# A graph-attention layer on one core: the row of reciprocal deviations goes through DRAM

## The chip, the core and the metric

The kernel runs on one core of a Trainium2 chip. A core has five engines that run their own instruction streams in order and meet through semaphores: TensorE (PE in the profile: matrix products and transposes, results in PSUM banks), VectorE (DVE), ScalarE (ACT), GpSimd (POOL) and SyncE (SP, which only issues transfers here). Sixteen DMA engines move data between DRAM and the on-chip memory SBUF, which has 128 partitions. The metric is the device time of one execution in microseconds (us); lower is better. The median before is 299.23 us over 3 runs (299.14 to 299.44).

## The reference

A graph layer on 384 nodes with 1024 features, 16 heads of 64. What matters here is its head, the layer norm and the three projections:

```python
h = jnp.maximum(_layernorm(x, axis=-1), 0.0)      # (x - mean) / sqrt(var + 1e-5), then relu
q = h @ wq.T + bq;  k = h @ wk.T + bk;  v = h @ wv.T + bv
q2 = (q @ wiq.T + biq)...;  k2 = (k @ wik.T + bik)...;  v2 = (v @ wiv.T + biv)...   # per head
mask = full((N, N), -inf); mask[src, dst] = softplus(edge_type_weights)[edge_type - 1]; diagonal filled
attn = softmax(q2 @ k2.T / 8 + mask);  out = attn @ v2
return x + (out @ wo.T + bo)
```

There are 6528 edges with types 0 to 4. Everything is float32.

## The kernel before

**Precision.** Each float32 operand is split into a rounded high part and a low part, and a product is three matmuls: high by high, high by low, low by high (`mm3`, L367). `split_hi` (L67) makes the high part of a weight chunk on ACT, `split_lo` (L79) the low part on DVE, or on POOL where one is named.

**Layer norm without its division.** The norm is taken apart. `ln_bn` and `ln_mean` (L246, L249) make mean and variance on DVE, `ln_sub` subtracts the mean, and PE transposes the centred rows, so that nodes lie along the free axis; relu and split give `hT`. The division by the standard deviation is left out at that point. Since relu commutes with a positive factor, it can be multiplied in later, on the result of each projection. `ln_root` and `ln_rstd` (L255, L259) make the reciprocal deviation, three columns of 128 (one for each block of nodes; node on the partition). `ln_row` (L266) turns these three columns into a row of 384 that is the same in all partitions, `rrow`: PE transposes each column, read as if it stood 128 times side by side, into one PSUM bank, and ACT copies the bank to SBUF. `evac_row` (L387) then multiplies the PSUM result of a chunk by `rrow` on DVE (L389), ACT adds the bias and rounds (L390), and DVE makes the low part (L391), put off to the next chunk's head by the list `post`.

**Chunks.** The work is a list of 56 weight chunks of 512 KB, numbered by `w`: 0 to 7 are the eight output blocks of v, 8 to 15 those of q, then the inner projection of v, k, and so on. A chunk takes 24 matmuls of 128x384. `slot_head(w)` (L402) runs ahead of each chunk: it splits the high part of chunk w+2 (ACT), empties `pend` (the evacuation of the chunk before), splits the low part of chunk w+2 (DVE), empties `post`, and issues the load of chunk w+5 on SP. `raw` has four buffers, so a load can start once the chunk four before it has been split.

**The first two chunks.** Their matmuls are written out as pieces, because the parts of `hT` and of the weights come in one after the other: chunk 0 high by high, then low by high; in the slot of chunk 1 its high by high, the rest of chunk 0, its low by high, and its high by low in two halves, with `ln_row` and the evacuation of chunk 0 (`flush`) between the halves (L422 to L429). PSUM has eight banks; the tag "g", in which chunks accumulate, has three, so chunk 3 takes chunk 0's bank once its evacuation has read it.

**The mask, beside it.** The mask is built from the edge list by POOL, DVE and DMA while the projections run. `softplus_a`, `softplus_b`, `softplus_c` (L155 to L167) make the four edge weights, `mask_values` (L169) the value of every edge on POOL. `detect(s)` (L442) is called behind each chunk of v and q: it clears one of three tables in DRAM (`table_clear`, L143, a transfer of 576 KB) behind the first three chunks, loads rows of keys, compares them for repeated edges (`mask_detect`, L213, on DVE), makes indices (`mask_index`) and, from the fourth on, scatters two columns of edges at a time (L224, POOL). `softplus_c` and `mask_values` are called by `detect(0)`.

**Order.** All engines' orders are as written in the program, and SP issues every transfer named here in one queue. An instruction that waits holds up all behind it on its engine.

Of the kernel before, what the change touches and what calls it, by code (L numbers as in the profile page):

```python
# [8 lines left out]
F32 = mybir.dt.float32  # L9
F32R = mybir.dt.float32r  # L10
I32 = mybir.dt.int32
AF = mybir.ActivationFunctionType
OP = mybir.AluOpType

N, D, NT, KT, NP = 384, 1024, 3, 8, 8
# [7 lines left out]
def gnn_kernel(ctx: ExitStack, tc: tile.TileContext, x, edges, erows, etw, wq, wk, wv, wiq, wik, wiv, wo,  # L23
# [6 lines left out]
    nc = tc.nc  # L30
# [5 lines left out]
    dram = ctx.enter_context(tc.tile_pool(name="dram", bufs=1, space=bass.MemoryType.DRAM))  # L36
# [7 lines left out]
    def bank(tag):  # L44
        return psum.tile([128, 512], F32, tag=tag, name=tag, bufs={"g": 3, "a": 1}.get(tag, 2))
# [14 lines left out]
    def load(w):  # L60
        if w >= NCH:
            return
        n, m = chunks[w]
        raw[w] = wpool.tile([128, D], F32, tag="raw", name="raw", bufs=4)
        nc.sync.dma_start(raw[w], W[n][m])

    def split_hi(w, dst=None, dve=False):  # L67
        if w >= NCH:
            return
        if dst is None:  # L70
            t = wpool.tile([128, 2, D], F32R, tag="whl", name="whl", bufs=4)
            dst = (t[:, 0, :], t[:, 1, :])
        whl[w] = dst
        if dve:
            nc.vector.tensor_copy(dst[0], raw[w])
        else:
            nc.scalar.activation(dst[0], raw[w], AF.Copy)  # L77

    def split_lo(w, eng=None):  # L79
        if w < NCH:  # L80
            hi, lo = whl[w]
            (eng or nc.vector).tensor_tensor(lo, raw[w], hi.bitcast(F32), OP.subtract)  # L82
# [24 lines left out]
    ident = const.tile([128, 128], F32, name="ident")  # L107
# [35 lines left out]
    def table_clear(g):  # L143

        nc.sync.dma_start(tabs[g][:CELLS, :].rearrange("(j p m) o -> p j (m o)", p=128, m=N),
                          zero[:, None, :].to_broadcast([128, NT, N]))
# [18 lines left out]
    def softplus_c():  # L165
        nc.vector.tensor_tensor(w8[:, 4:8], w8[:, 4:8], w8[:, 0:4], OP.add)
        nc.vector.tensor_scalar(w8[:, 4:8], w8[:, 4:8], 8.0, 1.0e-37, op0=OP.mult, op1=OP.max)  # L167

    def mask_values():  # L169
        t, ty = tmpe[:, 0, :], tmpe[:, 2, :]  # L170
        nc.gpsimd.tensor_scalar(val, ty, 0.0, w8[:, 7:8], op0=OP.is_equal, op1=OP.mult)
        for i in range(4):
            nc.gpsimd.tensor_scalar(t, ty, float(i + 1), w8[:, 4 + i:5 + i], op0=OP.is_equal, op1=OP.mult)
            nc.gpsimd.tensor_tensor(val, val, t, OP.add)
# [17 lines left out]
    def key_load(g, s):  # L192

        if s == 0:
            t = work.tile([128, 2, NT, N], F32R, tag="pt", name="rows")
            krv[g] = t.bitcast(F32).rearrange("p a k n -> p (a k n)")
        c0, c1 = parts(g)[s]
        dst = krv[g][:, s * PA * 128:(s * PA + c1 - c0) * 128]
        for c in range(c0, c1):
            rows[c] = krv[g][:, (s * PA + c - c0) * 128:(s * PA + c - c0 + 1) * 128]  # L200
        nc.sync.dma_start(dst, krow[c0:c1, :].rearrange("c j -> (c j)").partition_broadcast(128))
# [37 lines left out]

    hT = gtile("g1")  # L240
    lnt = work.tile([128, N], F32, tag="e", name="lnt", bufs=EB)
    var, negm, root, vq, inv, rstd = (lnt[:, c:c + NT] for c in (4, 8, 12, 16, 20, 24))
    var = lnt[:, 1:2 * NT:2]
    rrow = work.tile([128, 2, N], F32R, tag="qs", name="rrow").bitcast(F32)[:, 0, :]

    def ln_bn(t, h):  # L246
        nc.vector.bn_stats(lnt[:, 30 + 12 * t + 6 * h:36 + 12 * t + 6 * h], xt[t][:, h * 512:(h + 1) * 512])  # L247
# [18 lines left out]
    def ln_row():  # L266

        ps = bank("t")
        for t in range(NT):
            nc.tensor.transpose(ps[:, t * 128:(t + 1) * 128], rstd[:, t:t + 1].to_broadcast([128, 128]), ident)  # L270
        nc.scalar.activation(rrow, ps[:, :N], AF.Copy)

    def ln_sub(t, c0, c1, eng):
        src, dst = xt[t][:, c0:c1], xn[t][:, c0:c1]
# [97 lines left out]
    def colmm(ps, w, src, k):  # L372
        hi, lo = whl[w]
        mm3(ps[:, :N], hi[:, k * 128:(k + 1) * 128], lo[:, k * 128:(k + 1) * 128],
            src[:, 0, k, :], src[:, 1, k, :], k == 0, k == KT - 1)

    def pieces(ps, w, src, a, b, ks, n=(0, N)):

        for k in ks:
            nc.tensor.matmul(ps[:, n[0]:n[1]], whl[w][a][:, k * 128:(k + 1) * 128], src[:, b, k, n[0]:n[1]],  # L380
                             start=(a == b == k == n[0] == 0), stop=(b == 1 and k == KT - 1))
# [5 lines left out]
    def evac_row(ps, hi, lo, bias):  # L387
        f = work.tile([128, N], F32, tag="e", name="f", bufs=EB)
        nc.vector.tensor_tensor(f, ps[:, :N], rrow, OP.mult)  # L389
        nc.scalar.activation(hi, f, AF.Identity, bias=bias)  # L390
        post.append(lambda: nc.vector.scalar_tensor_tensor(lo, f, bias, hi.bitcast(F32), op0=OP.add, op1=OP.subtract))  # L391

    w = 0
    pend, post = [], []

    def flush(last=False):
        while pend:
            pend.pop(0)()
        while last and post:
            post.pop(0)()  # L400

    def slot_head(w):  # L402
        if w > 0:
            split_hi(w + 2)
        if w != 1:
            flush()
        split_lo(w + 2)
        while post:
            post.pop(0)()
        load(w + 5)  # L410

    def proj(src, dst, bidx, extra=None):
        nonlocal w
        for m in range(8):
            slot_head(w)
            ps = bank("g")
            if w == 0:
                ps0 = ps
                pieces(ps0, 0, src, 0, 0, range(KT), (0, 256))
                pieces(ps0, 0, src, 0, 0, range(KT), (256, N))  # L420
                pieces(ps0, 0, src, 1, 0, range(KT))
            elif w == 1:  # L422
                pieces(ps, 1, src, 0, 0, range(KT))
                pieces(ps0, 0, src, 0, 1, range(KT))
                pieces(ps, 1, src, 1, 0, range(KT))
                pieces(ps, 1, src, 0, 1, range(4))
                ln_row()
                flush()
                pieces(ps, 1, src, 0, 1, range(4, KT))  # L429
            else:  # L430
                for k in range(KT):
                    colmm(ps, w, src, k)
            pend.append(lambda ps=ps, m=m: evac_row(ps, dst[:, 0, m, :], dst[:, 1, m, :],
                                                bc[:, bidx * 8 + m:bidx * 8 + m + 1]))
            if extra:
                extra(m)
            w += 1

    def extra_v(m):
        detect(m)  # L440

    def detect(s):  # L442

        if s == 0:
            softplus_c()
            mask_values()
        if s < NTAB:
            table_clear(s)
        if 3 <= s < 6:
            key_load(1, s - 3)  # L450
        if 9 <= s < 12:
            key_load(2, s - 9)
        detects((0, 3, 6)[s] if s < 3 else 2)
        if s >= 3:
            scatters(2)
        if s == 14:
            biv_load()
# [3 lines left out]
    def detects(n):  # L461
        for i in range(nde[0], min(EC, nde[0] + n)):
            mask_detect(sc_order[i])
            if i + 1 == NTAB * JI[1]:
                mask_index(JI.pop(0), JI[0])
            nde[0] = i + 1

    def extra_q(m):
        detect(8 + m)
# [3 lines left out]
    def scatters(n):  # L473
        for _ in range(n):
            if nsc[0] < EC:
                mask_scatter(nsc[0])
                nsc[0] += 1
# [3 lines left out]
    def biv_load():  # L481
        t = work.tile([128, 2, 2, N], F32R, tag="ks", name="bivt")
        bivs["b"] = t.bitcast(F32).rearrange("p a k n -> p (a k n)")[:, 0:D]
        nc.sync.dma_start(bivs["b"], biv.partition_broadcast(128))

    vT = gtile("g2")
    proj(hT, vT, 2, extra_v)
    qT = gtile("g3")
    proj(hT, qT, 0, extra_q)

    xbd = dram.tile([N, D], F32, name="xbd")
# [24 lines left out]
    for k in range(8):  # L516
        slot_head(w)
        hi, lo = whl[w]
        for t in range(NT):
            for h in range(2):  # L520
                mm3(accs[t * 2 + h], vT[:, 0, k, t * 128:(t + 1) * 128], vT[:, 1, k, t * 128:(t + 1) * 128],
                    hi[:, h * 512:(h + 1) * 512], lo[:, h * 512:(h + 1) * 512], k == 0, k == KT - 1)
        detects(2)
        scatters(2)
        if k == 6:
            mask_fill()
            mask_base()
        if k >= 2:
            residual(k - 2)
        w += 1  # L530
# [11 lines left out]
    def extra_k(m):  # L542
# [5 lines left out]
        if m < 2:  # L548
            residual(m + 6)
    kT = gtile("g2")  # L550
    proj(hT, kT, 1, extra_k)
    flush(True)

# [332 lines left out]
```

## Time and profile before

| | us |
|---|---|
| median of 3 runs (lowest, highest) | 299.23 (299.14, 299.44) |
| the profiled execution | 298.95 |
| its span, first to last instruction | 297.2 |
| PE busy | 291.2 (98%) |
| DVE busy | 202.4 (68%) |
| POOL busy | 155.7 (52%) |
| ACT busy | 153.8 (52%) |
| packets of DMA queue q1, share of 16 engines' span | 56.0% |

Times in a timeline are counted from the span's start. A line of a timeline reads: start, duration, engine, line of the program, operation, output<-inputs, shapes, and in brackets how long the engine had been idle and what ended that. SPq lines are the issues of transfers; their duration is the issue alone, not the transfer. A transfer's end is seen where somebody waited for it. Numbers of buffers are left out of names: `g` stands for PSUM banks of the tag "g" and for the large tiles of activations, `raw` for loaded weights, `whl` for their high and low parts, `tab` for the tables. In a line of windows come the stretch, its length, busy time and number of instructions of each engine, the clock granted to PE, the mean busy share of the DMA engines and GB/s. The chain of waits is followed back from the last instruction; what stands on it decides the end.

### The profile page before, as it was taken

To read this page: it belongs to the slowest core of one execution; us is meant where nothing else is said; L and a number is where in the kernel's file an instruction comes from. 1 tells how busy PE (TensorE), PEld (TensorE's weight loads), DVE (VectorE), ACT (ScalarE), POOL (GpSimd) and SP (SyncE) were. 2 spreads that over 40 slices of the span, in tenths; PEclk is the share of its full clock that TensorE was granted. 3 is DMA by queue.
4 is the path that set the end of the run, shared out by engine and by line. 5 is a ranking of instruction groups with operands and counts; after the bars stand their busy time and mean duration, and the time that the engine had idled before them with its cause. 6 is when DMAs were issued, how large, how long until landed. Compare 5 with 4: busy or idle time off the path is not lost.

```text
span 297.2 us, 4982 instructions
## 1 busy us (share of the span) xinstructions
PE 291.2 (98%) x1654; PEld 276.5 (93%) x1654; DVE 202.4 (68%) x495; ACT 153.8 (52%) x288; POOL 155.7 (52%) x160
## 2 busy tenths in 40 slices
PE   6999999999999999999999999999999999999995
PEld 5999999999988889999999999999999998888884
DVE  4958977766856553888865676868686766696423
ACT  3784644433422222554336677778777767865310
POOL 3774567363857785710033656373746467976210
PEclk9999999999999999999999999999999999999999
DMA  7899864645396648393369784738374656900005
GB/s 279 277 324 398 292 207 131 225 143 212 116 303 202 197 153 289 113 342 112 117 167 261 206 216 115 202 93 223 99 221 121 170 144 176 348 10 0 2 3 209
DMA packets 22377, 55.12 MB, mean 185 GB/s; under 512 B 4816, under 2 KB 8400, under 8 KB 22352
## 3 DMA queue, kind: packets, MB, share of 16 engines
q1 hardware_dynamic: 19968, 52.42, 56.0%
q0 software_dynamic: 2064, 1.80, 2.1%
q10 hardware_dynamic: 320, 0.59, 0.9%
q8 instruction: 13, 0.21, 0.3%
q14 instruction: 12, 0.10, 0.1%
HBM read 40.39 MB, written 4.97 MB: 153 GB/s over the span
## 4 chain that ended last, share of the span: by engine, by line
PE 96%; DVE 1%; DMA 1%; ACT 0%; issue 0%
PE g L370 21%; PE g L368 21%; PE g L369 21%; PE a L758 6%; PE s L721 6%; PE t L741 5%; PE g L380 3%; PE s L369 2%; PE s L370 2%; PE s L368 2%; PE t L370 2%; PE t L369 2%; PE t L368 2%; DMA g<-in_x_dram 1%; DVE lnt L247 1%; PE a L369 1%
## 5 line engine op out<-in xcount | busy, mean ns | idle before, releaser
L368 PE MATMUL g<-g,whl 128*128 128x384 f32 x304 | 103.6, 341 | 0.0
L370 PE MATMUL g<-g,whl 128*128 128x384 f32 x304 | 101.8, 335 | 0.0
L369 PE MATMUL g<-g,whl 128*128 128x384 f32 x304 | 101.5, 334 | 0.0
L224 POOL DMA_INDIRECT tab<-val,idx x51 | 56.1, 1100 | 37.5 <-issue 11.0
L77 ACT ACTIVATE whl<-raw 128x1024 fp32r<-128x1024 f32 x51 | 53.6, 1051 | 29.7 <-PE g L370 21.1
L82 DVE TENSOR_TENSOR whl<-raw,whl 128x1024 fp32r<-128x1024 f32 x41 | 52.6, 1282 | 15.6 <-ACT whl L77 12.4
L736 POOL TENSOR_TENSOR e<-e,s 128x384 f32<-128x384 f32 x48 | 39.3, 829 | 43.1 <-DVE s L735 42.4
L369 PEld LDWEIGHTS g<-g,whl 128*128 128x128 f32 x304 | 57.2, 188 | 0.0
L368 PEld LDWEIGHTS g<-g,whl 128*128 128x128 f32 x304 | 57.1, 188 | 0.0
L370 PEld LDWEIGHTS g<-g,whl 128*128 128x128 f32 x304 | 57.0, 188 | 0.0
L82 POOL TENSOR_TENSOR whl<-raw,whl 128x1024 fp32r<-128x1024 f32 x11 | 26.4, 2398 | 30.8 <-ACT whl L77 28.1
L390 ACT ACTIVATE g<-f,bc 128x384 fp32r<-128x384 f32 x24 | 14.8, 618 | 52.7 <-DVE f L389 41.2
L751 DVE TENSOR_TENSOR pt<-t,pt 128x384 fp32r<-128x384 f32 x48 | 26.4, 549 | 15.3 <-ACT pt L750 15.0
L731 ACT ACTIVATE e<-e,s 128x384 f32<-128x384 f32 x48 | 29.2, 608 | 9.3 <-DVE s L727 8.1
L750 ACT ACTIVATE pt<-t 128x384 fp32r<-128x384 f32 x48 | 23.3, 486 | 13.6 <-PE t L741 13.3
L727 DVE CUSTOM_DVE_ANT_0 e<-s,ma 128x384 f32<-128x384 f32 x48 | 26.4, 549 | 3.6 <-PE s L721 3.4
L721 PE MATMUL s<-ks,qs 128*128 128x384 f32 x96 | 24.7, 338 | 0.0
L741 PE MATMUL t<-ident,e 128*128 128x128 f32 x144 | 23.5, 271 | 0.0
L389 DVE TENSOR_TENSOR f<-g,rrow 128x384 f32<-128x384 f32 x24 | 13.3, 556 | 13.9 <-PE g L370 13.7
L741 PEld LDWEIGHTS t<-ident,e 128*128 128x128 f32 x144 | 18.7, 140 | 3.1
L758 PE MATMUL a<-pt,vhl 128*128 128x384 f32 x96 | 20.8, 351 | 0.0
L721 PEld LDWEIGHTS s<-ks,qs 128*128 128x128 f32 x96 | 17.5, 188 | 0.8
(145 smaller groups left out, 416.2 us busy)
## 6 DMA issues: line engine op xcount, KB each, us to landing
ks<-nat SPq DMA_DIRECT2D x30, 192.0 KB
raw<-in_wv_dram SPq DMA_DIRECT2D x8, 512.0 KB
raw<-in_wq_dram SPq DMA_DIRECT2D x8, 512.0 KB
raw<-in_wiv_dram SPq DMA_DIRECT2D x8, 512.0 KB
raw<-in_wk_dram SPq DMA_DIRECT2D x8, 512.0 KB
raw<-in_wiq_dram SPq DMA_DIRECT2D x8, 512.0 KB
raw<-in_wik_dram SPq DMA_DIRECT2D x8, 512.0 KB
raw<-in_wo_dram SPq DMA_DIRECT2D x8, 512.0 KB
```

The source lines that it names most:

```text
L77: nc.scalar.activation(dst[0], raw[w], AF.Copy)
L82: (eng or nc.vector).tensor_tensor(lo, raw[w], hi.bitcast(F32), OP.subtract)
L224: nc.gpsimd.indirect_dma_start(out=tabs[c // RNG], out_offset=bass.IndirectOffsetOnAxis(ap=idx[:, c:c + 1], axis=0), in_=val[:, c:c + 1], ...
L368: nc.tensor.matmul(ps, lhi, rhi, start=first, stop=False)
L369: nc.tensor.matmul(ps, lhi, rlo, start=False, stop=False)
L370: nc.tensor.matmul(ps, llo, rhi, start=False, stop=last)
L721: nc.tensor.matmul(ps[:, :N], qs[:, o, t * 128:(t + 1) * 128], ks[:, o, s, :], start=(s == 0), stop=(s == 1))
L727: nc.vector.tensor_tensor_reduce(e, st_ps.pop(i)[:, :N], ma[:, t, :], -0.125, 3.0e38, OP.add, OP.min, s[:, 0:1])
L731: nc.scalar.activation(es[i], es[i], AF.Exp, bias=s[:, 0:1], scale=-1.0, accum_out=s[:, 1:2])
L736: nc.gpsimd.tensor_tensor(es[i], es[i], s[:, 2:3].to_broadcast([128, N]), OP.mult)
L741: nc.tensor.transpose(ps[:, k * 128:(k + 1) * 128], es[i][:, k * 128:(k + 1) * 128], ident)
L758: nc.tensor.matmul(ps[:, :N], vhl[:, k, p, 2 * o:2 * o + 2, :], pts[h][:, s, k, :], start=(k == 0 and s == 0), stop=(k == 2 and s == 1))
```

## The change

`ln_row` is made in another way, it stands eight matmuls earlier, and some work that was given out ahead of it or behind it is given out right behind it.

- The three reciprocal columns go to columns 128 to 130 of the small tile `lnt`; columns 128 to 255 are cleared on POOL at the start.
- `ln_row` transposes this 128x128 block once on PE. Its first three rows are copied by DVE from PSUM to SBUF (3x128), written to a DRAM tile `rdram` (1.5 KB), and read back from there into all 128 partitions of `rrow` (192 KB). Both transfers are issued by SP, the second after the first has landed. The copy by ACT (L271) is gone.
- It is called when four of the eight low-by-high matmuls of chunk 1 are given out, and no longer between the halves of the high-by-low ones.
- `softplus_c` and `mask_values` are called there, behind it, and no longer by `detect(0)`.
- The low part of chunk 3 (`split_lo(3)`) and the load of chunk 6 (`load(6)`) are given out there too, and no longer in `slot_head(1)`, which ends after the high part of chunk 3. The evacuation of chunk 0 stays where it was.

In program order this gives, on SP: load of chunk 5, clear of table 0, write of `rdram`, read of `rrow`, load of chunk 6, clear of table 1, load of chunk 7, clear of table 2. On DVE: low part of chunk 2, the 3x128 copy, the two softplus instructions, low part of chunk 3, multiplication of chunk 0 by `rrow`, three comparisons.

```diff
-    var, negm, root, vq, inv, rstd = (lnt[:, c:c + NT] for c in (4, 8, 12, 16, 20, 24))
+    var, negm, root, vq, inv, rstd = (lnt[:, c:c + NT] for c in (4, 8, 12, 16, 20, 128))
     var = lnt[:, 1:2 * NT:2]
     rrow = work.tile([128, 2, N], F32R, tag="qs", name="rrow").bitcast(F32)[:, 0, :]
+    rdram = dram.tile([NT, 128], F32, name="rdram")
+    nc.gpsimd.memset(lnt[:, 128:256], 0.0)
...
     def ln_row():
 
         ps = bank("t")
-        for t in range(NT):
-            nc.tensor.transpose(ps[:, t * 128:(t + 1) * 128], rstd[:, t:t + 1].to_broadcast([128, 128]), ident)
-        nc.scalar.activation(rrow, ps[:, :N], AF.Copy)
+        nc.tensor.transpose(ps[:, :128], lnt[:, 128:256], ident)
+        nc.vector.tensor_copy(lnt[:NT, 256:384], ps[:NT, :128])
+        nc.sync.dma_start(rdram, lnt[:NT, 256:384])
+        nc.sync.dma_start(rrow, rdram.rearrange("t n -> (t n)").partition_broadcast(128))
...
     def slot_head(w):
         if w > 0:
             split_hi(w + 2)
-        if w != 1:
-            flush()
+        if w == 1:
+            return
+        flush()
         split_lo(w + 2)
         while post:
             post.pop(0)()
...
             elif w == 1:
                 pieces(ps, 1, src, 0, 0, range(KT))
                 pieces(ps0, 0, src, 0, 1, range(KT))
-                pieces(ps, 1, src, 1, 0, range(KT))
+                pieces(ps, 1, src, 1, 0, range(4))
+                ln_row()
+                softplus_c()
+                mask_values()
+                split_lo(3)
+                load(6)
+                pieces(ps, 1, src, 1, 0, range(4, KT))
                 pieces(ps, 1, src, 0, 1, range(4))
-                ln_row()
                 flush()
                 pieces(ps, 1, src, 0, 1, range(4, KT))
...
     def detect(s):
 
-        if s == 0:
-            softplus_c()
-            mask_values()
         if s < NTAB:
             table_clear(s)
```

## The prediction

> **What bounds the kernel now.** I read the page's busy shares and its chain first. TensorE (PE) is busy 291.2 of 297.2 us and the chain is 96% PE. Then I read the chain in order of time for the edited place:
>
> ```profile
> PE 291.2 (98%) x1654; PEld 276.5 (93%) x1654; DVE 202.4 (68%) x495; ACT 153.8 (52%) x288; POOL 155.7 (52%) x160
> ...
> 10.41 8.16 PE g L380 x52
> 18.57 0.33 PE t L270 x3
> 18.89 0.71 PE g L380 x4
> ```
>
> From 10.4 us on, PE runs without a pause, so any instruction taken off PE is a gain and any wait put in front of PE is a loss of the same size. The three transposes of the edited function cost 0.33 us on the chain, 0.11 each. The next view is the timeline of PE around the first matmul that needs the edited row in time:
>
> ```profile
> 23.44 0.33 PE L370 MATMUL g<-g,whl 128*128 128x384 f32 x1
> 23.61 0.33 PE L368 MATMUL g<-g,whl 128*128 128x384 f32 x1
> ```
>
> 23.61 is the first matmul of chunk 3. There are three "g" banks, chunks 0, 1 and 2 hold them, so chunk 3 needs chunk 0's bank back. That bank is freed by the multiplication with the reciprocal row, L389 on DVE:
>
> ```profile
> 15.63 1.21 DVE L82 TENSOR_TENSOR whl<-raw,whl 128x1024 fp32r<-128x1024 f32 x1
> 17.97 0.16 DVE L166 TENSOR_TENSOR w<-w 128x4 f32<-128x4 f32 x1 [1.14 <-ACT w L161]
> ...
> 20.44 1.22 DVE L82 TENSOR_TENSOR whl<-raw,whl 128x1024 fp32r<-128x1024 f32 x1 [2.10 <-ACT whl L77]
> 21.58 0.55 DVE L389 TENSOR_TENSOR f<-g,rrow 128x384 f32<-128x384 f32 x1
> ```
>
> It ends at 22.13, so the row has 1.48 us to spare before 23.61. Now the row will come through DMA, so I read what SP's queue does there, when it issues and when others get what it issued:
>
> ```profile
> 12.70 2.70 SPq L65 DMA_DIRECT2D raw<-in_wv_dram  x2
> 15.45 0.89 SPq L145 DMA_DIRECT2D tab<-zero  x1
> 16.87 0.34 SPq L65 DMA_DIRECT2D raw<-in_wv_dram  x1
> 17.26 0.54 SPq L145 DMA_DIRECT2D tab<-zero  x1
> ```
>
> ```profile
> 23.34 1.06 ACT L77 ACTIVATE whl<-raw 128x1024 fp32r<-128x1024 f32 x1 [0.56 <-DMA raw<-in_wv_dram]
> 28.76 0.98 POOL L224 DMA_INDIRECT tab<-val,idx  x1 [0.73 <-DMA tab<-zero]
> ```
>
> The first row holds the loads of chunks 4 (12.70) and 5 (15.06). Chunk 4, issued at 12.70, is only there at 23.34: 10.6 us. The second table clear, issued at 17.26, is there at 28.76: 11.5 us. Between them the queue holds chunk 5, table 0, chunk 6 and table 1, 2 x 0.524 + 2 x 0.590 = 2.23 MB, in 5.42 us: 411 GB/s. The windows agree that the DMA engines are full:
>
> ```profile
> 15.00:18.00 3.00, 3.00 (x19) 3.00 (x18) 1.80 (x7) 2.94 (x5) 1.81 (x4) 1.00 1.03 255
> 18.00:21.00 3.00, 3.00 (x20) 2.96 (x19) 0.87 (x3) 2.77 (x4) 2.28 (x5) 1.00 1.00 359
> 21.00:24.00 3.00, 3.00 (x20) 3.00 (x19) 2.14 (x9) 1.28 (x2) 2.40 (x5) 1.00 1.04 400
> 24.00:27.00 3.00, 3.00 (x19) 3.00 (x18) 2.99 (x6) 1.97 (x3) 0.29 (x1) 1.00 1.05 409
> ```
>
> The last two columns are the DMA engines' share (1 is full) and GB/s. So the changed kernel puts two dependent transfers into a queue that is some ten microseconds deep.
>
> **The change part by part.**
>
> *PE.* Two of three transposes go: 0.22 us off the chain. The one left stands eight matmuls earlier: 18.41 - 8 x 0.174 = 17.0, after the reciprocals (15.53), so it waits for nothing. The cleared columns are a 128x128 memset on POOL; one such at 1.33 took 0.20 us, and POOL next has work at 5.73 after 3.15 idle: nothing.
>
> *ACT and DVE.* ACT loses L271 (0.47), with 1.39 idle behind it: nothing. DVE gains a 3x128 copy, between its rows of 128x4 (0.17) and 128x384 (0.55), put at 0.3. It runs from 17.3 in DVE's idle 1.14 before L166, ends about 17.6, and delays nothing. Softplus end and edge values keep their releaser (ACT's logarithm, ending 17.94), so their move costs nothing; nor does that of chunk 3's low part, released by ACT at 20.40 as before. It still stands ahead of the multiplication on DVE, so chunk 3's weights are ready at 21.66.
>
> *The write of the row.* SP issues it about 17.6, behind chunks 4 and 5 and table 0. Upper bound of its landing: the last DMA engine is through with chunk 4 at 23.34, then with 1.11 MB more at 0.405 MB per us, 2.75 us: 26.1. Lower bound: SP had issued 6.67 MB up to and with table 0, and the windows have moved that sum at 22.6, so an average engine is done then. (For chunk 4 the same sum gives 19.7 against 23.34 seen: some engines lag by 3.7.) I take 26.1, because each wait in this stretch ended with the last engine.
>
> The Trainium skill (DMA: Bandwidth & Descriptors, "Why a DMA increments its semaphore by 16 and not by 1") says that such a DMA runs only on as many engines as divide its slowest dimension, three for three rows, and counts only these. No row here has so few rows to show it; by the page the write would land with those three engines, early unless one of them lags, and the sum would be near 302.8 instead.
>
> *The broadcast read.* SP waits for the write before it issues this. Issue to use, nearest rows: the small store of the keys, 8.78 to 10.69, 1.91 us, and a 256 KB store whose follower waits for it, 90.10 to 92.83, 2.73 us. I take the middle, 2.3. So the row is there at 26.1 + 2.3 = 28.4. Ends: 28.8 at 2.73; and 26.6 if the write lands early, since the read has 128 rows and still queues behind table 0 on the lagging engines (26.1, plus its own 0.2 MB, 0.5 us).
>
> *What then waits.* DVE's multiplication starts 28.4, ends 28.95, PE starts chunk 3 about 29.0 in place of 23.61: **5.4 us** (3.6 to 5.8). PE would have been free at 23.4, so the 0.22 saved goes into the pause.
>
> *What is queued behind the two waits.* On SP, chunk 6, table 1, chunk 7 and table 2 wait behind the read: issued from about 26.5 in place of 16.87. Chunk 6 is used 8.43 us after the multiplication (30.01 against 21.58), so now at 36.8, ten microseconds after its issue into an emptied queue (the first load of such a size took 3.3): nothing. Scatters start 5.1 after it (26.71), now 33.5; table 1's clear, 0.2 + 0.52 + 0.59 MB after 26.2, is there by 32: nothing. On DVE three comparisons, an index pair, chunk 1's multiplication and the low parts of chunks 4 and 5 wait. From L389's start to the end of chunk 5's low part DVE took 30.58 - 21.58 = 9.00, of which 0.83 was a wait for POOL's edge values, done by then: 8.17. PE reaches chunk 5 0.6 + 2 x 4.17 = 8.93 after the row. So DVE is in time by 0.76 us, and no second stop follows. ACT, behind its bias step, has chunk 4's high part in time for DVE by about 0.1.
>
> Sum: +5.4 against the profiled run's 298.95, which lies 0.28 under the median of 299.23: **304.6 us** by the median.
>
> **The rivals.**
>
> *The row comes by fewer engines (302.8).* Same stop, but the write lands at 22.6 to 24 and only the read is held by the lagging engines: row at 26.6, chunk 3 at 27.2, +3.6. For it: three rows are few. Against it: nothing in the trace has fewer than all.
>
> *The stop also costs TensorE its pace (306.5).* At the start PE runs 20 transposes in 4.27 us, later three in 0.49: the slow stretch lost about 4.27 - 20 x 0.11 = 2 us. A PE pause of 0.98 us (before 6.68) did not bring the slow pace back; one of 3.7 to 5.6 is not in the trace. Bounds 0 and 2 us, so 304.6 + 1.9.
>
> The Trainium skill (TensorE: Matmul & The Clock Gate, "Part 1: The HAM clock gate") has PE fall to half clock after an idle window of about 3.4 us that runs free. By it a pause of 5.6 us holds a whole window about two times in three, and one of 3.7 hardly ever.
>
> *The other side: the small transfers pass the queue (299.0).* If the write and the read took 1.9 us each, as the keys' store did, the row would be there at 21.4, DVE would start at 21.66 as before, and only the 0.22 us gain is left. It decides at: row by 22.8, so both transfers within 5.2 us of 17.6, where their neighbours take 10.4 and 11.5. Against it: the keys' store had 0.2 MB ahead of it (2.77 issued, 2.6 moved), and the read must use engines that are still busy with chunk 4 at 23.
>
> **How the numbers follow.** In-order stop at full pace 0.40, 304.6 (its own range 304.2 to 305.1, by 1.91 and 2.73 for the read); fewer engines 0.27, 302.8; slow pace after the stop 0.26, 306.5 (from 304.7 to 307); passing the queue 0.05, 299.0; something worse, such as DVE missing chunk 5 too, 0.02. The range 302.3 to 307.0 leaves out the last two and the far end of the slow pace. About 0.2%, 0.6 us, is what can be told from no change: the passing case (-0.2) is mostly within it. Faster 0.01, same 0.04, slower 0.95.
>
> **What would show it.** Right: DVE idle from 21.7 to 26 or later before the first L392 with a DMA of the row as releaser; a PE gap of 3.5 to 5.6 us before chunk 3; SP's broadcast read issued 22.7 to 26.2, chunk 6's load right behind it; no other PE gap until 285. The transposes of PE would take 0.11 instead of 0.33. Matmul spacing after the gap tells the pace: 0.174 is full, about 0.35 slow. Wrong: the read issued before 20.5, or a row that lands within 5 us of 17.6; also a second stop at chunk 5, 6 or 7.

## The result, and the profile after

The changed kernel takes 307.38 us (median of 4 runs, 307.09 to 307.65) against 299.34 before: a ratio of 1.026, 95% interval 1.0244 to 1.0277. It is slower by 8.0 us where 5.4 were forecast, and 0.4 us above the top of the range. The profiled execution is the one of 307.65, span 305.9.

The page's first lines and its row of the clock granted to TensorE, in 40 slices of 7.6 us:

```profile
PE 294.8 (96%) x1652; PEld 280.2 (92%) x1652; DVE 202.2 (66%) x496; ACT 153.6 (50%) x287; POOL 156.0 (51%) x161
...
PEclk9998799999999999999999999999999999999999
```

PE has two instructions fewer and is busy 3.6 us longer: somewhere it works slower. The clock row says where, slices four and five (22.9 to 38.2 us). The chain of waits between 18 and 34 us, start and length of each piece:

```profile
18.45 0.12 PE t L271
18.60 0.04 DVE lnt L272
...
18.91 6.06 DMA rdram<-lnt
24.98 4.72 DMA rrow<-rdram
29.73 0.57 DVE f L392
30.30 0.14 issue
30.43 0.66 PE g L371
31.09 0.32 PE g L372
```

Before, this stretch of the chain was PE alone. Now it leaves PE for the two transfers and comes back through the multiplication. What SP issued, and how long DVE stood:

```profile
18.91 0.33 SPq L273 DMA_DIRECT2D rdram<-lnt  x1
24.98 0.34 SPq L274 DMA_DIRECT2D rrow<-rdram  x1
25.42 0.38 SPq L65 DMA_DIRECT2D raw<-in_wv_dram  x1
```

```profile
29.73 0.56 DVE L392 TENSOR_TENSOR f<-g,rrow 128x384 f32<-128x384 f32 x1 [7.40 <-DMA rrow<-rdram]
```

And PE's timeline around the stop:

```profile
24.50 0.34 PE L373 MATMUL g<-g,whl 128*128 128x384 f32 x1
30.43 0.66 PE L371 MATMUL g<-g,whl 128*128 128x384 f32 x1 [5.59 <-DVE f L392]
30.89 0.52 PE L372 MATMUL g<-g,whl 128*128 128x384 f32 x1
31.21 0.52 PE L373 MATMUL g<-g,whl 128*128 128x384 f32 x1
...
34.41 0.40 PE L371 MATMUL g<-g,whl 128*128 128x384 f32 x1
34.65 0.33 PE L372 MATMUL g<-g,whl 128*128 128x384 f32 x1
34.83 0.33 PE L373 MATMUL g<-g,whl 128*128 128x384 f32 x1
```

Starts lie 0.173 apart before 24.50 and after 34.65, and 0.32 between. From these rows the two executions' spans can be set against each other. Chunk 3 would have begun at 24.50 + 0.17 = 24.67, 1.06 later than the 23.61 of before. The stop is 30.43 - 24.67 = 5.76 (the 5.59 in the bracket is counted from the last matmul's end, 24.84; "idle" below is counted like that). The 13 matmuls from 30.43 to 34.65 took 4.22 in place of 13 x 0.1735 = 2.26, so the slow pace cost 1.96. Together 8.78, where the spans differ by 305.9 - 297.2 = 8.7. Nothing is lost after 35 us, and nothing is won back.

The 1.06 comes from the start of the run and not from the edited place. In this execution the third block of x came 0.7 us later (its statistics start at 7.85 in place of 7.14), and the first transposes kept the slow pace of the start until 10.3 us, so chunk 0's first matmul is at 11.50 in place of 10.16. Whether the change has to do with that is asked below.

### The profile page after: what moved, and what is told of

Read it like the earlier page. It is cut to its first block, busy times and chain, and to the rows that moved or that the text cites. A ratio compares the mean times of both kernels' runs of the same rounds, so it can differ in the third digit from the quotient of the medians.

```text
span 305.9 us, 4984 instructions
## 1 busy us (share of the span) xinstructions
PE 294.8 (96%) x1652; PEld 280.2 (92%) x1652; DVE 202.2 (66%) x496; ACT 153.6 (50%) x287; POOL 156.0 (51%) x161
## 4 chain that ended last, share of the span: by engine, by line
PE 93%; DMA 5%; DVE 1%; ACT 0%; issue 0%
PE g L371 20%; PE g L373 20%; PE g L372 20%; PE a L764 6%; PE s L727 6%; PE t L747 5%; PE g L383 2%; DMA rdram<-lnt 2%; PE s L372 2%; PE s L373 2%; PE s L371 2%; DMA rrow<-rdram 2%; PE t L373 2%; PE t L372 2%; PE t L371 1%; DMA g<-in_x_dram 1%
## 5 line engine op out<-in xcount | busy, mean ns | idle before, releaser
L371 PEld LDWEIGHTS g<-g,whl 128*128 128x128 f32 x304 | 57.8, 190 | 5.9 <-issue 5.9
L372 PEld LDWEIGHTS g<-g,whl 128*128 128x128 f32 x304 | 57.8, 190 | 0.0
L373 PEld LDWEIGHTS g<-g,whl 128*128 128x128 f32 x304 | 57.6, 190 | 0.0
```

Of the source, the lines that this page charges most:

```text
L371: nc.tensor.matmul(ps, lhi, rhi, start=first, stop=False)
L372: nc.tensor.matmul(ps, lhi, rlo, start=False, stop=False)
L373: nc.tensor.matmul(ps, llo, rhi, start=False, stop=last)
```

## Experiments

Two theories of the loss. **The wait**: only the time from the write's issue to the read's landing counts, by a stop of PE before chunk 3, and the slow pace follows from that stop. **Rivals**: the moved work costs something; the loads that SP holds back behind the read cost something; the slow pace has a cause of its own. Within the wait, what makes the write and the read take 6.1 and 4.7 us is asked separately. In the three groups of runs the kernel before took 299.71, 299.80 and 299.55 us, and each ratio is to the kernel before of its own group.

### Is it the way through DRAM, and there the wait alone?

**Moves without the way through DRAM** (e1_moves_only): `ln_row` as before, all else as changed.

```diff
-        nc.tensor.transpose(ps[:, :128], lnt[:, 128:256], ident)
-        nc.vector.tensor_copy(lnt[:NT, 256:384], ps[:NT, :128])
-        nc.sync.dma_start(rdram, lnt[:NT, 256:384])
-        nc.sync.dma_start(rrow, rdram...partition_broadcast(128))
+        for t in range(NT):
+            nc.tensor.transpose(ps[:, t * 128:(t + 1) * 128], rstd[:, t:t + 1].to_broadcast([128, 128]), ident)
+        nc.scalar.activation(rrow, ps[:, :N], AF.Copy)
```

> The changed kernel with the row made as before (three transposes, ACT copies them), everything else moved as in the change. Theory (the way through DRAM is the whole loss): TensorE does not stop at chunk 3, 299.3 us, within 0.3 of before. Rival (the moves cost a part, for one the 0.6 us that the stop and the slow pace leave unexplained): 299.9 or more.

Measured: ratio 1.0003 (0.9989 to 1.0016), 299.95 us over 12 runs, no stop of PE behind 11 us. The moved softplus, edge values, low part and load, and the memset, cost nothing.

**The way through DRAM without the moves** (e2_route_only): the kernel before with the new `ln_row` at the old place.

> The kernel before with the row made by one transpose and sent through DRAM, at its old place: now the load of chunk 6 and the clear of table 1 (1.11 MB) are issued ahead of the write. Theory (the write waits in order for all that stands ahead in SP's queue): it lands 1.11 MB at 0.405 MB per us, 2.7 us, later than in the changed kernel; the stop is 2.7 us longer, 310 us. Rival (the loads that SP holds back behind the read are what costs): they are not all held back here, so less than 307.

Measured: 306.5 us, 1.0207 (1.0179 to 1.0234), PE stopped for 5.5. The loss is there without the moves, which with the run before it settles where it sits. The number of the expectation was wrong by a slip: the clear of table 1 is given out behind chunk 1, so behind the row's transfers, and only chunk 6's load stood ahead. The chain:

```profile
23.03 3.10 DMA rdram<-lnt
26.15 3.14 DMA rrow<-rdram
29.31 0.57 DVE f L393
```

The write is issued 4 us later than in the changed kernel (the copy waits on DVE behind chunk 3's low part) and lands after 3.1, at 26.15 in place of 24.98, so later, as the theory has it. But the read takes 3.1 in place of 4.7: the row comes at about the same time (29.3 and 29.7) by another division.

**The trip made, but not waited for** (e8_trip_unused): write and read go into a spare tile, and the row is made as before.

```diff
-        nc.sync.dma_start(rrow, rdram...partition_broadcast(128))
+        nc.sync.dma_start(rother, rdram...partition_broadcast(128))
+        for t in range(NT):
+            nc.tensor.transpose(ps[:, t * 128:(t + 1) * 128], rstd[:, t:t + 1].to_broadcast([128, 128]), ident)
+        nc.scalar.activation(rrow, ps[:, :N], AF.Copy)
```

> The changed kernel with write and read of the row still made, into a tile that nobody uses, and the row itself made as before by three transposes and ACT. Theory (only the wait for the read's landing costs): no stop at chunk 3, 299.7 us, as before on this chip. Rival (SP's held-back loads, or the traffic, cost by themselves): a stop of TensorE or a wait for a weight chunk later on, over 300.5.

Measured: 1.0002 (0.9991 to 1.0013), 299.79 us over 10 runs. SP issued chunk 6's load only at 24.56, 7.7 us later than in the profile of before, and PE did not stop at chunk 3:

```profile
18.27 0.33 SPq L274 DMA_DIRECT2D rdram<-lnt  x1
24.12 0.34 SPq L275 DMA_DIRECT2D rother<-rdram  x1
24.56 0.38 SPq L65 DMA_DIRECT2D raw<-in_wv_dram  x1
```

So neither the traffic nor the held-back loads cost anything. It is the wait alone.

### The slow pace

**The changed kernel again** (after_again), for the other runs to stand beside.

> The changed kernel unaltered, so that the others of this group stand beside it on one chip. 307.4 us. If the 0.6 us that stop and slow pace left over come from the start of the run (arrival of the input, pace of the first transposes), the place of the first chunk's matmuls will differ from the first profile's 11.5 us and the total with it, by 1.3 us at most.

Measured: 307.27 us, 1.0241 (1.0194 to 1.0288); the profiled execution (306.72) has a write of 4.54, a read of 4.72, a stop of 4.24 (idle 4.07) and 2.6 lost to the slow pace. Its first matmul of chunk 0 stands at 11.50 again, so this run alone doesn't answer the question of the start; others do, below.

**PE kept busy during the stop** (e4_busy_stop).

```diff
+                if w == 2:
+                    keep = bank("a")
+                    for i in range(48):
+                        nc.tensor.transpose(keep[:, :128], ident, ident)
```

> The changed kernel with 48 transposes of the identity into an unused bank behind chunk 2, 5.2 us of work that nobody reads, inside the stop of 5.8 us. Theory (TensorE runs at half pace after the stop because it stood idle): the matmuls after the stop are 0.174 us apart at once and 2.0 us are gained, 305.4. Rival (the slow pace has another cause, such as a limit on what the chip grants): 307.4 or more.

Measured: 305.51 us, 1.020 (1.018 to 1.022), 1.8 less than the changed kernel (1.7 to 2.2 less, each set against the kernel before of its own group). The row still came at 27.85, and the matmuls behind are at full pace at once:

```profile
23.23 0.34 PE L373 MATMUL g<-g,whl 128*128 128x384 f32 x1
23.41 5.40 PE L445 MATMUL a<-ident 128*128 128x128 f32 x48
28.57 0.42 PE L371 MATMUL g<-g,whl 128*128 128x384 f32 x1
28.83 0.34 PE L372 MATMUL g<-g,whl 128*128 128x384 f32 x1
29.00 0.34 PE L373 MATMUL g<-g,whl 128*128 128x384 f32 x1
```

The clock granted behind the stop (third number from the end) is 1.00, where the changed kernel has 0.51; first e4, then the changed kernel:

```profile
28.50:32.70 4.20, 4.20 (x27) 4.20 (x26) 4.05 (x15) 3.08 (x4) 1.83 (x1) 1.00 1.05 377
```

```profile
30.40:34.60 4.20, 4.17 (x13) 4.20 (x14) 4.05 (x15) 3.04 (x4) 1.83 (x1) 0.51 1.06 375
```

The mean clock of a whole execution says the same: 0.998 to 1.000 in all six of e4, 0.987 to 0.994 in all eight of the changed kernel. Work that nobody reads bought 1.8 us: the slow pace comes of standing idle.

**A stop with no transfer** (stop_dve3, stop_dve4, stop_dve6): the kernel before with additions on DVE ahead of chunk 0's multiplication.

```diff
                 ln_row()
+                scratch = ma.rearrange("p a n -> p (a n)")[:, :768]
+                for i in range(3):                       # 4, 6
+                    nc.vector.tensor_tensor(scratch, xt[0][:, :768], xt[0][:, 256:1024], OP.add)
                 flush()
```

> The kernel before, no transfer added, with three additions of 128x768 (0.86 us each) on DVE ahead of chunk 0's multiplication, 2.6 us, of which 1.5 are spare: a stop of TensorE of 1.1 us and nothing else. If the slow pace needs a stop longer than this, 299.8 + 1.1 = 300.9; if not, 302.5 to 303.

> The same with four additions, a stop of 2.0 us. If a stop of 2 us costs the pace as the one of 2.4 us in the shallow-queue run did, 299.8 + 2.0 + 2 = 303.8; if only a stop of a whole 3.4 us does, 301.8.

> The same with six additions, a stop of 3.7 us, about that of the changed kernel but without any transfer. Theory (stop and pace explain the change's loss, the transfers nothing beside them): 299.8 + 3.7 + 2.2 = 305.7, with slow matmuls behind the stop. Rival (the slow pace comes with the transfers): 303.5.

| run | PE idle at chunk 3 | pace behind it | median us | ratio (95%) |
|---|---|---|---|---|
| stop_dve3 | 1.3 | full | 301.16 | 1.0058 (1.0037 to 1.0079) |
| stop_dve4 | 2.4 | full (profiled execution) | 302.53 | 1.0112 (1.0075 to 1.0148) |
| stop_dve6 | 4.4 | half | 306.58 | 1.0239 (1.0204 to 1.0274) |

An addition took 1.0 and not 0.86, so the stops came out longer than planned. The jump is between the second and the third: 2.0 us more of idling, 4.0 us more of time. The pace is not settled by the length of the stop alone: of the four executions of stop_dve4 one (303.69 us) has a mean clock of 0.994, the others 0.998 to 1.000. By estimate, half pace for 3.4 us lowers the mean of 302 us by 0.006, so that one seems to have had it. The two windows' rows in the profiled executions, behind a stop of 2.4 (stop_dve4) and of 4.4 (stop_dve6), with the clock as the third number from the end:

```profile
26.90:31.00 4.10, 4.08 (x23) 4.08 (x24) 3.95 (x13) 3.14 (x4) 1.84 (x1) 1.00 0.76 269
```

```profile
29.20:32.30 3.10, 3.08 (x10) 3.08 (x11) 2.95 (x11) 2.85 (x4) 0.89 (x1) 0.50 0.07 23
```

With no transfer added, a stop as long as the changed kernel's costs nearly what the change costs: 7.0 of 7.5 to 8.0 us.

### What makes the transfers long

**Less ahead of the write** (e3_shallow_queue): chunk 5's load and table 0's clear go behind the row's transfers.

```diff
-        load(w + 5)
+        if w > 0:
+            load(w + 5)
...
+                load(5)
+                table_clear(0)
                 load(6)
...
-        if s < NTAB:
+        if 0 < s < NTAB:
```

> The changed kernel with the load of chunk 5 and the clear of table 0 given out behind the row's two transfers in place of ahead of them: 1.11 MB less ahead of the write. Theory (queue order): the write lands with chunk 4, some 2.7 us sooner, the stop is 3 us; whether the slow pace still follows is open: 302.7 without it, 304.7 with it. Rival (the write and the read have a fixed price, whatever is queued): 307.4 as before, or later, since chunk 5 comes later.

Measured: 302.94 us, 1.0089 (1.0059 to 1.0119), runs between 299.99 and 304.51. The chain:

```profile
18.35 2.79 DMA rdram<-lnt
21.16 4.62 DMA rrow<-rdram
25.80 0.57 DVE f L392
```

The write takes 2.8 in place of 4.5 to 6.1: what was handed to the DMA engines earlier does stand ahead of it. The read is as long as ever. PE stood 2.2 us, and in the profiled execution the slow pace came all the same, from the third matmul on:

```profile
26.51 0.41 PE L371 MATMUL g<-g,whl 128*128 128x384 f32 x1 [2.23 <-DVE f L392]
26.76 0.48 PE L372 MATMUL g<-g,whl 128*128 128x384 f32 x1
27.04 0.52 PE L373 MATMUL g<-g,whl 128*128 128x384 f32 x1
27.36 0.52 PE L371 MATMUL g<-g,whl 128*128 128x384 f32 x1
```

So 2.2 us can be enough, where 2.4 in the profiled stop_dve4 was not. The traces' record of the clock tells the two apart. In every trace here the clock changes only at the ends of steps of 3.41 us: it is full for five, six or seven of them before it falls (17.07, 20.48 or 23.89 us), and half for one or two (3.41 or 6.83). What differs is how much of one step PE stood idle. In e3 all 2.23 us lay in the step that ended at 26.80; in stop_dve4 a step ended within the stop, at 25.12, and split its 2.36 us into 0.56 and 1.80. The steps, first e3, then stop_dve4 (length, then PE's busy time):

```profile
23.39:26.80 3.41, 1.18 (x8) 0.89 (x7) 1.00 (x4) 0.40 (x1) 1.06 (x3) 1.00 0.78 262
26.80:30.21 3.41, 3.41 (x12) 3.41 (x11) 3.26 (x10) 2.73 (x4) 0.78 (x1) 0.50 1.06 412
```

```profile
25.12:28.53 3.41, 1.61 (x9) 1.61 (x10) 3.23 (x12) 1.57 (x2) 1.34 (x2) 1.00 1.02 399
28.53:31.94 3.41, 3.41 (x22) 3.41 (x21) 3.41 (x13) 1.57 (x2) 2.53 (x2) 1.00 0.65 204
```

In the seven profiles in which the clock fell behind the stop, PE was idle for 2.23 to 3.41 us of the step before; in no profile did it stay full behind a step with more than 1.80 idle. So for stops of this length it is chance where the steps lie: by their mean clocks, five of e3's ten executions had the slow pace (0.992 to 0.994, 303.39 to 304.51 us) and five had not (0.998 to 1.000, 299.99 to 302.50).

**POOL's queue** (e6_pool_queue): both transfers issued by POOL.

```diff
-        nc.sync.dma_start(rdram, lnt[:NT, 256:384])
-        nc.sync.dma_start(rrow, rdram...partition_broadcast(128))
+        nc.gpsimd.dma_start(rdram, lnt[:NT, 256:384])
+        nc.gpsimd.dma_start(rrow, rdram...partition_broadcast(128))
```

> The changed kernel with both of the row's transfers issued by POOL, whose queue holds nothing else yet, so that SP holds back no loads. Theory (what delays the write is its place behind SP's loads): the write lands within 3 us of its issue in place of 4.5 to 6, the read still meets the loads on the DMA engines, 4 to 5 us; the row is there 2 to 3 us sooner, about 304 to 305. Rival (the engines are full, so any queue waits as long): 307 or more.

Measured: 308.54 us, 1.030 (1.0269 to 1.0331), slower than the change. The theory as put there fell:

```profile
18.48 6.07 DMA rdram<-lnt
24.86 5.31 DMA rrow<-rdram
```

A queue of its own did not bring the write through sooner. But the run does not show that the place in SP's queue counts for nothing: as SP was free, it issued chunk 6's load and table 1's clear at 17.45 and 17.84, ahead of the write and not behind it. In the trace the write's three packets run from 22.44 to 23.01, while chunk 6 lands from 24.45 to 26.22 and table 1 from 25.92 to 27.65, so the write passed 1.11 MB that SP had given out before it. Two things held it all the same. Its packets start four microseconds after the issue; those of SP's write in the changed kernel do so too (issue 18.91, packets from 22.68 to 24.48). And the trace has sixteen landings for POOL's write, the last at 24.56, where SP's has three. Why the packets start so late stays open.

**128 different rows** (e5_distinct_rows): the read fetches a full 128x384 tile of DRAM.

```diff
-    rdram = dram.tile([NT, 128], F32, name="rdram")
+    rdram = dram.tile([128, N], F32, name="rdram")
...
-        nc.sync.dma_start(rdram, lnt[:NT, 256:384])
-        nc.sync.dma_start(rrow, rdram...partition_broadcast(128))
+        nc.sync.dma_start(rdram[0:1, :].rearrange("o (t n) -> (o t) n", t=NT), lnt[:NT, 256:384])
+        nc.sync.dma_start(rrow, rdram)
...
+    nc.sync.dma_start(rdram, zero)
     key_rows()
```

> The changed kernel with the read fetching 128 different rows of 1.5 KB from a DRAM tile of that size, cleared early by one more transfer of 192 KB, in place of the same 1.5 KB for all 128 partitions (only partition 0 gets the true row, so the result changes). Theory (128 reads of the same 1.5 KB hinder each other): read issue to landing 2.3 to 3 us in place of 4.7, the stop 1.7 to 2.4 us shorter, 305.0 to 306. Rival (the read is slow because the loads of chunk 6 and table 1 come right behind it in the queue): 4.7 us and 307.4 or more.

**Nothing behind the read** (e7_nothing_behind): chunk 6's load waits until the row has been used.

```diff
-                load(6)
...
                 flush()
+                raw[6] = wpool.tile([128, D], F32, tag="raw", name="raw", bufs=4)
+                nc.vector.memset(raw[6][:, 0:1], 0.0)
+                nc.sync.dma_start(raw[6], W["v"][6])
```

> The changed kernel with the load of chunk 6, and so all that SP issues later, held until the row has been used (one column of its buffer is cleared behind the multiplication): nothing stands behind the read. Theory (same address): the read still takes 4.7 us, 307.4. Rival (what follows it in the queue): the read takes 2.3 to 3.1 us, the stop is 1.6 us or more shorter, 305 to 306; chunk 6 then lands about 3.5 us after the row, ahead of its use 8.4 us after it.

Measured: e5 302.72 us, 1.0105 (1.0077 to 1.0132); e7 306.3 us, 1.0206 (1.0161 to 1.025). The reads on the chain, first e5, then e7:

```profile
18.86 4.18 DMA rdram<-lnt
23.06 2.44 DMA rrow<-rdram
```

```profile
17.62 6.46 DMA rdram<-lnt
24.10 3.20 DMA rrow<-rdram
```

Each of the two ideas, one address and the loads behind, holds in part. With the loads right behind it, the read takes 2.4 us from different rows and 4.6 to 4.7 from one row read 128 times (both profiles of the changed kernel, e3). With nothing behind it, the same row takes 3.2; in e2, with a table's clear issued 0.4 us and a weight load 0.9 us behind it, 3.1. So reading one address 128 times was slow where a weight load was issued 0.44 us behind it; that a load as such is enough, e2 speaks against, and whether its nearness or the order counts was not tested. e5 gained more than expected, 4.6 us: in the profiled execution (301.48) its stop of 1.4 us did not cost the pace, though the mean clocks of 0.994 and 0.992 say that two of the four (303.13 and 303.57) did have it. e7 gained only 1.0: its write took 6.46 (why is not shown), and its stop of 4.5 still cost the pace.

## Why the prediction was wrong

- **Bound and place: right.** PE is the bound, chunk 3 is where the row is needed, DVE waits in order, SP's loads behind the read cost nothing (e8), ACT and DVE's added copy and the moves cost nothing (e1), and no second stop comes, at chunk 5 or later.
- **The write: too long.** 8.5 us were put down (issue at 17.6, landing at 26.1); it took 4.2 to 6.5 in the changed kernel and its variants with the same queue. The landing at 26.1, taken as that of the last engine through with table 0, was wrong in two ways. The last engine was through at 24.1 to 25.2 in these runs (25.8 in the profile of before). And the write does not wait for all engines: the trace has three packets of 512 bytes for the write and the landings of three engines, as the rule of the Trainium skill (DMA: Bandwidth & Descriptors, "Why a DMA increments its semaphore by 16 and not by 1") gives for a slowest dimension of three, and in the second profile of the changed kernel the read is issued at 23.45, before the last engine is through with table 0 at 25.2. In the first profile one of the three was as late as the last of all (24.97 and 24.98), so the three engines did not always help.
- **The read: too short.** 2.3 was taken from stores; 4.7 was measured. Neither row had many engines read one address. The two errors nearly cancel, by luck: 10.8 us forecast for the trip, 10.8 and 9.3 measured. The stop of 5.4 to 5.6 forecast was 5.76 and 4.24.
- **The pace: the step that failed.** The main sum put it at nothing; it stood as a rival with 0.26, priced 1.9 from the slow transposes of the start. The price was near (1.96 and 2.6; 1.5 to 2.7 over the seven profiles that show it, where the bound was 2), in part by luck, since a slow stretch is one or two steps of 3.41 us less what the stop itself covers. The chance was wrong: all six profiled executions with 4.1 us or more of idling (4.07 to 6.79) show the slow pace. The sum of that rival, 306.5, is 0.9 below the result, and the range's top, 307.0, had cut off its far end. From the trace of before the chance could not be read, since its longest pause of PE was 1.0 us; the Trainium skill's rule (TensorE: Matmul & The Clock Gate, "Part 1: The HAM clock gate", an idle window of about 3.4 us) spoke, by the prediction's estimate from it, for two in three at the forecast stop, and should have weighed more.
- **The rest.** Stop and slow pace, less the 0.22 saved, make 7.5 and 6.6 of the 8.0 and 7.5 by which the medians differ. The start of the run differs between executions by up to 1.3 us: chunk 0 begins at 10.16 in the one profile of before, at 11.50 in both of the changed kernel, but at 10.20 in e4 and 10.15 in e7, which have the changed kernel's start to the letter, and at 10.55 in e1, which has it too and is no slower than before. The record of the clock goes with it: full from 10.65 and 10.46 in the changed kernel's two profiles, from 6.61 in e4, 6.45 in e7, 5.83 in e1 and 5.22 before. So the start is not the change's doing; whether it accounts for the whole remainder was not shown.
- **The other rivals.** The transfers did not pass the queue (299.0; of the neighbours' times given there, chunk 4's is 10.6, as read further up, and not 10.4). Fewer engines for the write was right as a mechanism, but did not shorten the trip, for the read took back what the write gave.

## What to carry to other kernels

A round trip through DRAM that ends in front of the bounding engine is to be priced by the data already handed to the DMA engines, plus a read that can be slowed by the loads issued right behind it, here 9 to 11 us for 1.5 KB; it is free only if nobody waits (e8). A stop of TensorE costs its own length. From some 2 us on it can cost about 2 us again, and all six of 4.1 us or more did, because the matmuls behind it run at half pace: price both, or fill the stop with work. When a waiting instruction stands in front of the bounding engine, look first at the spare time it had before, here 1.5 us against a trip that no queue in the trace had made in less than 1.9 for one leg.

## What was not expected of the hardware

- Half pace can follow a stop of only 2.2 us (e3) and did not follow one of 2.4 (stop_dve4, profiled execution). The Trainium skill (TensorE: Matmul & The Clock Gate, "Part 1: The HAM clock gate") puts the fall behind an idle window of about 3.4 us, which neither stop could fill; the measurement of e3 says that less can do. In the traces here it fell behind steps of 3.41 us with 2.23 us or more of idling and not behind those with 1.80 or less. In e3 it set in 0.29 us after PE had resumed (26.80 and 26.51), and lasted 3.41 us.
- One 1.5 KB row read into 128 partitions took 4.6 to 4.7 us with a weight load issued 0.44 us behind it, 3.1 to 3.2 in the two runs where none was so near (e2, e7), and 128 different rows with the load as near took 2.4 (e5).
- A write from POOL's otherwise empty queue took 6.1 us while SP's loads filled the engines, though its packets passed the last two transfers that SP had issued before it (e6).
